# Two graph layers on one core: the order of the first batch's weight work, the bias product, the last batch's key-block sums and the last two row scalings are changed

## The chip, the cores and the metric

The kernel runs on one core of a Trainium2 chip. The metric is the device time of one execution in microseconds (us); lower is better. The engines are named as in the profile: PE is TensorE (PEld its weight loads), DVE is VectorE, ACT is ScalarE, POOL is GpSimd, SP is SyncE, which here issues most DMAs. A name with a "q" (SPq, ACTq) is the engine's sequencer, where DMA issues and waits are counted.

## The reference

The input x is 32 batches of 512 rows of 512 values; adj is one 512x512 0/1 matrix for all batches. Two layers follow one another. A layer norm here has no learned scale, and a row is normalised over its 512 values.

```python
# layer 0, per batch (a = adj as float, deg = a.sum(axis=1))
mi = x @ Wi.T ; mj = x @ Wj.T
h = layernorm(x + deg[:, None] * (mi + b) + a @ mj)
# layer 1: masked attention with 8 heads of 64
q, k, v = h @ Wq.T + bq, h @ Wk.T + bk, h @ Wv.T + bv
s = where(adj == 0, -inf, q_h @ k_h.T / 8)     # per head
o = softmax(s) @ v_h                            # heads side by side
out = layernorm(h + o @ Wo.T + bo)
```

All data are float32.

## The kernel before

**Products.** Each 512x512 product is done in seven pieces instead of eight: the weight and the activation are cut into quarters, and sums and differences of quarters are multiplied (a Strassen-like scheme). `piece` (L442) does one product of such a pair on TensorE, on one of two PSUM banks, `mma` and `mmb`; piece 1 is copied by ScalarE into `p1` (L465), and piece 2 of v and of q accumulates on the same bank afterwards, so it waits for that copy. The sums and differences of the weights' quarters are made once, by `combine` (L280), part 0 and part 1 of each weight; they are stored to DRAM (L301), and come back into a ring of seven tiles, which `prefetch` (L310) loads in the order in which the pieces will use them (L313). Each `combine` takes buffers of the pools `e` (four), `es` (two), `xa` or `oT`. Batch 0's layer 0 does not use pieces: `plain` (L629) multiplies row block ic (128 rows, ic = 0 to 3) by the whole weights, eight products of 128x128 by 512.

**The start.** `first` (L616) is an order written out by hand for batch 0 until its v, q and k begin. Its steps issue to every engine in that order, and each engine runs its own instructions strictly in order. `y[ic]` is `plain(ic)`: TensorE's product, VectorE's addition into x (L637) and statistics (L325, L326), and three small GpSimd steps (L327 to L329) that make the scale and the shift of the layer norm. `scaled(ic)` is the layer norm's scaling of that block on ScalarE (L332). `n[ic]` (`l0_norm`, L378) transposes the block on TensorE; ScalarE copies it out (L385). `half("wk", i)` is part i of the combination of k's weight on VectorE. `graph_forms(0)` and `(1)` compare adj with its transpose and sum the difference, for a flag. `fold` (L703) puts v's bias into the output bias: since the weights of a softmax sum to one, bv passes through to the product with Wo, so bo becomes bo + bv @ Wo.T. Part 0 spreads each quarter of bv over 128 columns; part 1 multiplies these four 128x128 tiles with Wo, each with 512 columns, accumulated in one PSUM tile of the pool `ov`, and VectorE adds it to `bo_r`. Behind `first` comes `phase_c(0)`: v's and q's piece 1, v's piece 2, the transposes of blocks 2 and 3, and so on.

**The batches.** From there TensorE does, in 32 periods, the attention of batch n-1 interleaved with layer 0 and projections of batches n and n-2. Per period there are eight steps, head group g (0 or 1) by key block kc (0 to 3). In each step `scores` (L508) multiplies for two head pairs (i = 0, 1) into a PSUM tile `sc` (two buffers), ScalarE takes the exponential in place (L516), and `mask` (L518) multiplies it on VectorE by the 0/1 edges into a tile `e`, of which there are four. So a mask waits until its `e` buffer was read by everybody, and scores wait until their `sc` buffer was read by the mask. `values` (L531) multiplies the masked tiles with v, in 32-column tiles; the softmax denominators come from `presum` (L523), which adds the masked tiles of successive key blocks into `es`, and from `sums` (L541), products with ones in 32-column tiles. `presum(i, kc)` with kc = 1 is line L527, with larger kc L529.

**The last batch** (`alone` in the main loop) goes step by step with little else to do. Its presums are dealt out by

```python
late = [(f, i, c, (nc.gpsimd, nc.vector)[i == c - 1]) for f, i, c in late]
```

so that of the sums at kc = 1 pair 0's is VectorE's and pair 1's is GpSimd's, and at kc = 2 the other way round; at g = 1 there are only the sums at kc = 1. One of the waiting presums is issued after each todo of the step that counts as work (`late[:1]`).

**The end.** After the last sums, the denominators are inverted by columns, the attention output is scaled, and `last_part` (L753) multiplies with Wo; block 3's product starts from x itself. `last_rows(ic)` (L766) adds, takes statistics (`ln_stats`), scales on ScalarE (L773) and stores the block (L774). `flags` (L776) makes a number that says whether the general path below has to run; all engines load it at L913.

Of the kernel before, what the change touches and what calls it, by code (L numbers as in the profile page):

```python
# [13 lines left out]
AF = mybir.ActivationFunctionType  # L14
OP = mybir.AluOpType
AX = mybir.AxisListType

P = 128
# [7 lines left out]
def gnn_attention_kernel(  # L26
# [36 lines left out]
    nc = tc.nc  # L63
    B, N, D = x.shape
    NC = N // P
    DC = D // P
# [13 lines left out]
    def work(shape, name, bufs, dtype=FT):  # L80
        return pools.work.tile(shape, dtype, name=name, bufs=bufs)
# [4 lines left out]
    def mm_tile(bank):  # L86
        return psum.tile([P, 512], FT, name="mm" + bank, bufs=1)

    def ov_tile():
        return psum.tile([P, 512], FT, name="ov", bufs=2)  # L90
# [10 lines left out]
    XT, XA, XD, AX_T, HT, MV = {}, {}, {}, {}, {}, {}  # L101
# [3 lines left out]
    def rows(ap):  # L105
        return ap.rearrange("(c p) d -> p c d", p=P)
# [35 lines left out]
    W = {}  # L142
# [9 lines left out]
    ones = const.tile([P, P], FT, name="ones")  # L152
# [77 lines left out]
    pd = mm_tile("b")  # L230
# [89 lines left out]
        return t  # L320


    def ln_stats(mv, y):
        st = work([P, 6], "st", 4)
        nc.vector.bn_stats(st, y)  # L325
        nc.vector.bn_aggr(mv[:, 0:2], st)  # L326
        nc.gpsimd.tensor_scalar(mv[:, 2:3], mv[:, 1:2], EPS, 1.0, op0=OP.add, op1=OP.mult)  # L327
        nc.gpsimd.tensor_tensor(mv[:, 3:4], mv[:, 2:3], mhalf, OP.pow)
        nc.gpsimd.tensor_scalar(mv[:, 4:5], mv[:, 0:1], mv[:, 3:4], -1.0, op0=OP.mult, op1=OP.mult)  # L329

    def ln_apply(mv, y):
        nc.scalar.activation(y, y, AF.Identity, bias=mv[:, 4:5], scale=mv[:, 3:4])  # L332
# [98 lines left out]
    OPEN = {}  # L431
# [86 lines left out]
    def mask(hp, kc):  # L518
        ps = SC.pop(hp)
        e = E[hp % 2, kc] = work([P, 2, N], "e", 4)  # L520
        nc.vector.tensor_tensor(e, ps, edge[:, kc:kc + 1, :].to_broadcast([P, 2, N]), op=OP.mult)  # L521
# [58 lines left out]
    PC, TR, GA = 1.73, 0.44, 1.9  # L580
    FLUSH = (0.0, None)

    def z(f, *a):
        return (0.0, f, *a)

    def pc(kind, b, i, bank):
        return (2 * PC if kind == "l0" else PC, piece, kind, b, i, bank)
# [5 lines left out]
    def banks(n):  # L593

        return ("a", "b") if n % 2 == 0 else ("b", "a")
# [20 lines left out]
    def first():  # L616


        g = [(GA, l0_gather, 0, dc, "ab"[dc % 2]) for dc in range(DC)]
        t = [(TR, l0_xt, 0, dc) for dc in range(DC)]  # L620
        half = lambda name, i: z(combine, name, nc.gpsimd if name in ("wi", "wj") else nc.vector, i)
        y = [(8 * PC / 4, plain, ic) for ic in range(NC)]
        n = [(TR, l0_norm, 0, ic) for ic in range(NC)]
        return [g[0], t[2], g[1], t[3], z(graph_forms, 3), g[2], g[3], half("wi", 0), z(base, 0, range(2)), z(base, 0, range(2, 4)),
                half("wv", 0), z(load_bv), half("wi", 1), z(last_load), y[0], z(scaled, 0), half("wv", 1), z(prefetch), half("wq", 0), half("wj", 0),
                z(fold, 0), y[1], z(scaled, 1), half("wq", 1), half("wj", 1), y[2], half("wk", 0), z(graph_forms, 0), z(scaled, 2), n[0],
                y[3], half("wk", 1), z(prefetch), z(graph_forms, 1), n[1], (2 * PC, fold, 1), z(scaled, 3)]

    def plain(ic):  # L629

# [72 lines left out]
    def fold(part):  # L703

        if part == 0:
            bv_w = OPEN["fold"] = work([P, DC, P], "rl", 1)
            for dc in range(DC):
                nc.vector.tensor_scalar(bv_w[:, dc, :], ones, bv_c[:, dc:dc + 1], None, op0=OP.mult)
        else:
            pd = ov_tile()  # L710
            for dc in range(DC):
                nc.tensor.matmul(pd, OPEN["fold"][:, dc, :], W["wo"][dc // 2][:, dc % 2, :], start=(dc == 0), stop=(dc == DC - 1))
            nc.vector.tensor_add(bo_r, bo_r, pd)

    def by_steps(todo, half=None):
# [23 lines left out]
    def run(f):  # L739
        f[1](*f[2:])  # L740
# [6 lines left out]
    ACC = {}  # L747
# [15 lines left out]
            nc.tensor.matmul(ACC[ic], OT[B - 1, c // 2][:, c % 2, ic * P:(ic + 1) * P], W["wo"][c // 2][:, c % 2, :],  # L763
                             start=(c == 0 and ic < NC - 1), stop=(c == 3))

    def last_rows(ic):  # L766
        y = XT[B - 1][:, ic, :]
        mv = work([P, 5], "mv", 12)
        if ic < NC - 1:
            nc.vector.tensor_add(y, y, ACC[ic])  # L770
            ACC[ic] = y
        ln_stats(mv, ACC[ic])
        nc.scalar.activation(y, ACC[ic], AF.Identity, bias=mv[:, 4:5], scale=mv[:, 3:4])  # L773
        nc.sync.dma_start(rows(out[B - 1])[:, ic, :], y)  # L774

    def flags():  # L776

        pd = ov_tile()
        nc.tensor.matmul(pd[:, 0:1], ones, tot, start=True, stop=True)
        nc.vector.tensor_scalar(tot, pd[:, 0:1], SAFE, None, op0=OP.is_lt)  # L780
        nc.vector.tensor_scalar(again, tot, -1.0, 1.0, op0=OP.mult, op1=OP.add)

    PERIODS = [first() + phase_c(0) + phase_a(1)]
    half = None
    for n in range(1, B):
        todo = phase_b(n) + phase_c(n) + phase_a(n + 1)
        if n == 1:

            a, b, c = [todo.index(f) for f in (z(between, apply, 1, 0), pc("k", 1, 2, banks(1)[0]), phase_a(2)[0])]
            PERIODS += [[todo[:a], [], todo[a:b], [], todo[b:c], [], todo[c:], []]]  # L790
            continue
        if n < B - 1:
            half = sum(f[0] for f in todo) / 2
# [13 lines left out]
    for n in range(1, B + 1):  # L807
        b = n - 1

        alone = b == B - 1  # L810
        size = 1 if alone else 2
        for step in range(0, STEPS, size):
            g, kc = divmod(step, NC)
            extra = []
            for i in range(2):
                scores(b, 2 * g + i, kc)
            for f in due:
                values(*f)
            for i in range(2):
                mask(2 * g + i, kc)  # L820
            todo = [f for todo in PERIODS[n][step:step + size] for f in todo]
            while todo and todo[0][1] is between:
                run(todo.pop(0))
            if not due:

                run(todo.pop(0))
            if due and due[-1][2] == NC - 1:
                pb, pg = due[-1][:2]
                sums(pg, *(((1, 3), 3) if pb == B - 1 else ()))
                drain(pb, pg)  # L830
                extra = rest(pb, pg)
            due = [(b, g, kc + i) for i in range(size)]
            late = [(presum, i, c) for _, _, c in due if c > 0 for i in range(2)]
            if alone:

                late = [(f, i, c, (nc.gpsimd, nc.vector)[i == c - 1]) for f, i, c in late]
                if kc > 2 - g:

                    late = []
                if g == 1 and kc == 0:  # L840

                    for f in extra[:-1]:
                        f[0](*f[1:])
                    extra = extra[-1:]
                hold = False
            else:
                for i in range(2):
                    scores(b, 2 * g + i, kc + 1)
                for f in late if kc > 0 else []:

                    if f[2] == kc:
                        f[0](*f[1:])
                late = [(mask, 2 * g + i, kc + 1) for i in range(2)] + extra[-1:] + [f for f in late if f[2] > kc]

                for f in extra[:-1] if extra else late[:1]:
                    f[0](*f[1:])
                late, extra, hold = late[0 if extra else 1:], [], bool(extra) and g == 1
            for f in todo:
                if f is FLUSH:
                    some = len(extra)  # L860
                else:
                    run(f)

                    some = 0 if f[0] == 0.0 else len(extra) if step == 0 and alone else max(1, round(f[0] / PC))
                    if f[1] is piece and f[2] == "l0" and f[4] == 3:

                        some = 0
                    if some and hold:

                        some, hold = 0, False  # L870
                if some:
                    for g in late[:1] + extra[:some]:
                        g[0](*g[1:])
                    late, extra = late[1:], extra[some:]
            for g in late + extra:
                g[0](*g[1:])
    sums(1, (1, 2), 3)
    values(B - 1, 1, 3)
    sums(1, (3,), 3)
# [26 lines left out]
    nc.vector.reduce_sum(tot, told, axis=AX.X)  # L906
    last_part(2, ic=3)
    last_part(3, ic=3)
    last_rows(2)
    last_rows(3)  # L910
    flags()
    fast.close()
    flag = nc.values_load(again[0:1, 0:1], min_val=0, max_val=1)  # L913
    with tc.If(flag > 0), tc.tile_pool(name="general", bufs=1) as pools.work:
        wi, wj, wv, wq, wk, wo = [load_w(work([P, DC, D], f"w{i}", 1), src, nc.sync)
                                  for i, src in enumerate((wiT, wjT, wvT, wqT, wkT, woT))]
# [5 lines left out]
        pd = mm_tile("a")  # L922
# [22 lines left out]
        with tc.For_i(0, B, 1) as b:  # L945
            g = "general"
# [7 lines left out]
            for ic in range(NC):  # L954
                c = slice(ic * P, (ic + 1) * P)
# [10 lines left out]
            for ic in range(NC):  # L966
                c = slice(ic * P, (ic + 1) * P)
                nc.vector.tensor_copy(V[g][:, ic, :], product([(HT[g][:, dc, c], wv[:, dc, :]) for dc in range(DC)]))
            for hp in range(HP):
                c = slice(hp * P, (hp + 1) * P)  # L970
# [5 lines left out]
                for qb in range(NC):  # L976
# [7 lines left out]
                    for s in range(2):  # L984
# [3 lines left out]
                                            op0=OP.mult, op1=OP.add)  # L988
# [11 lines left out]
                    for kc in range(NC):  # L1000
                        for s in range(2):
                            c0 = hp * P + s * HD
                            nc.tensor.matmul(pm[s * HD:(s + 1) * HD, :P], V[g][:, kc, c0:c0 + HD], pT[:, s, kc, :],
                                             start=(kc == 0), stop=(kc == NC - 1))
                    nc.scalar.copy(OT[g, hp][:, qb * P:(qb + 1) * P], pm[:, :P])
            for ic in range(NC):
                c = slice(ic * P, (ic + 1) * P)
# [45 lines left out]
```

## Time and profile before

| | |
|---|---|
| timed runs | 3634.32, 3634.50, 3635.02, 3635.49 us; median 3634.76 |
| the profiled execution | 3637.43 us, its span 3635.7 us, mean granted TensorE clock 0.999 |
| busy share of the span | PE 100%, PEld 69%, DVE 65%, POOL 55%, ACT 28% |
| sum of presums on GpSimd, 128x1024 (L527) | 126 of 2.355 us |
| mask on VectorE, 128x1024 (L521) | 512 of 1.217 us |
| one float32 piece (8 passes of 128x256) | 1.73 us from one piece's start to the next's |
| scores of both pairs (8 passes of 64x512) | 1.92 us likewise |

A float32 product shows up as two passes on PE, so four products of the program are "x8" in the profile. The duration of a merged group of matmuls (1.89 for a piece) includes the last one's way through the array; what counts for the next one is the time from start to start. The timeline gives start, duration, engine, line and operation, tiles, and in brackets how long the engine had been idle and what ended that.

### The profile page before, as it was taken

The page shows a single profiled execution, that of the slowest core. Times are in us where ns is not written, and L with a number is a line of the kernel's source. Part 1 is how long each engine was busy: PE and PEld are TensorE (multiplying, and loading weights), DVE is VectorE, ACT ScalarE, POOL GpSimd, SP SyncE. Part 2 cuts the span into 40 slices and gives each one's busy share as a digit, 9 for nine tenths or more (in the row PEclk, how much of TensorE's full clock was granted, in tenths as well). Part 3 has the DMA queues.
Part 4 walks back from the last instruction along what each step waited for, and adds up shares of the span by engine and source line. Part 5 has one row for each costly group of instructions (what it writes and reads, how often), then busy time and mean ns, then how long its engine had stood idle before and what let it go on. Part 6 is the DMA issues. An engine that isn't in the chain of part 4 may idle for free.

```text
span 3635.7 us, 49789 instructions
## 1 busy us (share of the span) xinstructions
PE 3619.5 (100%) x18480; PEld 2525.3 (69%) x18480; DVE 2377.1 (65%) x3139; ACT 1035.8 (28%) x1486; POOL 2001.2 (55%) x1981
## 2 busy tenths in 40 slices
PE   9999999999999999999999999999999999999998
PEld 6677767776777667766776677667776777677764
DVE  5566666666766666666666666666666666666666
ACT  2322232222322222223223322232222222222222
POOL 4465654656456565455564465654656555565453
PEclk9999999999999999999999999999999999999999
DMA  8445555454555445554555545555554555455541
GB/s 266 139 125 142 145 148 162 143 137 138 145 162 153 132 136 147 157 161 119 146 146 154 160 131 140 144 145 163 146 135 136 148 160 153 131 139 145 159 134 56
DMA packets 797190, 530.02 MB, mean 146 GB/s; under 512 B 530448, under 2 KB 611856, under 8 KB 796944
## 3 DMA queue, kind: packets, MB, share of 16 engines
q1 hardware_dynamic: 779200, 493.73, 49.4%
q10 hardware_dynamic: 17520, 32.51, 2.5%
q8 instruction: 150, 2.46, 0.3%
q14 instruction: 96, 0.79, 0.1%
q0 software_dynamic: 224, 0.53, 0.0%
HBM read 453.25 MB, written 73.40 MB: 145 GB/s over the span
## 4 chain that ended last, share of the span: by engine, by line
PE 97%; DVE 1%; DMA 1%; POOL 1%; ACT 0%; issue 0%; SPq 0%; ACTq 0%; POOLq 0%; DVEq 0%
PE mma L458 32%; PE mmb L458 31%; PE sc L512 13%; PE ov L538 12%; PE mmb L356 3%; PE mma L356 3%; PE sc L548 2%; DMA xh<-in_x_dram 0%; DVE rl L557 0%; DMA b_r<-in_b_dram 0%; DMA wj<-e 0%; DVE xh L376 0%; DVE e L521 0%; POOL big L427 0%; DMA ring<-in_wvT_dram 0%; POOL es L527 0%
## 5 line engine op out<-in xcount | busy, mean ns | idle before, releaser
L521 DVE TENSOR_TENSOR e<-sc,edge 128x1024 f32<-128x1024 f32 x512 | 607.2, 1217 | 493.1 <-PE ov L538 481.5
L516 ACT ACTIVATE sc<-sc 128x1024 f32<-128x1024 f32 x512 | 495.2, 1007 | 902.6 <-PE sc L512 900.0
L458 PE MATMUL mmb<-ring,big 128*128 128x256 f32 x3144 | 728.4, 380 | 0.6 <-ACT big L385 0.6
L458 PE MATMUL mma<-ring,big 128*128 128x256 f32 x3112 | 721.0, 380 | 1.3 <-ACT p L465 1.3
L458 PEld LDWEIGHTS mmb<-ring,big 128*128 128x128 f32 x3144 | 594.5, 190 | 104.9 <-issue 24.3
L458 PEld LDWEIGHTS mma<-ring,big 128*128 128x128 f32 x3112 | 588.4, 190 | 105.3 <-issue 24.1
L427 POOL TENSOR_TENSOR big<-big 128x512 f32<-128x512 f32 x376 | 488.6, 1326 | 258.7 <-PE sc L512 234.4
L512 PE MATMUL sc<-q,k 64*128 64x512 f32 x2048 | 514.7, 621 | 2.6 <-DVE e L521 2.6
L538 PE MATMUL ov<-e,v 128*32 128x512 f32 x4096 | 467.6, 596 | 0.0
L190 POOL TENSOR_TENSOR xlo<-xh,xhi 128x512 fp32r<-128x512 f32 x127 | 161.7, 1284 | 533.5 <-ACT xhi L189 533.4
L458 PE MATMUL mma<-big,ring 128*128 128x256 f32 x1808 | 428.7, 380 | 0.0
L458 PE MATMUL mmb<-big,ring 128*128 128x256 f32 x1776 | 421.3, 380 | 0.0
L458 PEld LDWEIGHTS mma<-big,ring 128*128 128x128 f32 x1808 | 341.7, 190 | 60.1 <-issue 12.1
L458 PEld LDWEIGHTS mmb<-big,ring 128*128 128x128 f32 x1776 | 335.6, 190 | 59.9 <-issue 13.0
L512 PEld LDWEIGHTS sc<-q,k 64*128 64x128 f32 x2048 | 165.5, 185 | 287.9 <-DVE e L521 146.6
L327 POOL TENSOR_SCALAR mv<-mv 128x1 f32<-128x1 f32 x256 | 79.8, 312 | 516.9 <-DVE mv L326 504.6
L538 PEld LDWEIGHTS ov<-e,v 128*32 128x32 f32 x4096 | 119.8, 110 | 328.8 <-issue 327.3
L527 POOL TENSOR_TENSOR es<-e 128x1024 f32<-128x1024 f32 x126 | 295.3, 2355 | 57.9 <-DVE e L521 57.9
L529 DVE TENSOR_TENSOR es<-es,e 128x1024 f32<-128x1024 f32 x249 | 297.3, 1215 | 0.0
L473 POOL TENSOR_TENSOR xh<-xh,p 128x512 f32<-128x512 f32 x186 | 230.6, 1268 | 110.2 <-ACT p L465 110.2
L476 DVE TENSOR_TENSOR xh<-xh,mma 128x512 f32<-128x512 f32 x186 | 126.9, 682 | 190.8 <-PE mma L458 174.4
L476 DVE TENSOR_TENSOR xh<-xh,mmb 128x512 f32<-128x512 f32 x186 | 126.9, 682 | 189.9 <-PE mmb L458 173.4
(168 smaller groups left out, 3639.4 us busy)
## 6 DMA issues: line engine op xcount, KB each, us to landing
ring<-wo SPq DMA_DIRECT2D x217, 256.0 KB, 2.8
ring<-wq SPq DMA_DIRECT2D x160, 256.0 KB, 3.6
ring<-wv SPq DMA_DIRECT2D x160, 256.0 KB, 3.2
ring<-wk SPq DMA_DIRECT2D x160, 256.0 KB, 4.5
ring<-wi SPq DMA_DIRECT2D x155, 256.0 KB, 2.6
ring<-wj SPq DMA_DIRECT2D x155, 256.0 KB, 2.6
xh<-in_x_dram SPq DMA_DIRECT2D x31, 1024.0 KB, 6.1
xa<-in_x_dram SPq DMA_DIRECT2D x124, 256.0 KB, 4.3
```

The lines of the kernel that those rows point to most:

```text
L190: (by or nc.gpsimd).tensor_sub(lo, xs, hi.bitcast(FT))
L356: nc.tensor.matmul(pm, parts[w][:, jc, :], adjR[:, jc, :], start=(w == 0 and jc == 0), stop=(w == 1 and jc == NC - 1))
L427: nc.gpsimd.tensor_tensor(dst, p, q, op=OP.subtract)
L458: nc.tensor.matmul(pm[:, c * Q:(c + 1) * Q], lhs, rhs, start=first, stop=(kc == 1 and n == len(terms) - 1), skip_group_check=True)
L473: nc.gpsimd.tensor_tensor(d, d, p1, op=OP.add)
L476: nc.vector.tensor_tensor(d, d, pm, op=OP.add)
L512: nc.tensor.matmul(ps[:, s, :], KT[b, hp // 2][r, hp % 2, kc * P:(kc + 1) * P], QT[b, hp // 2][r, hp % 2, :], start=True, stop=True)
L516: nc.scalar.activation(ps, ps, AF.Exp, scale=QSCALE)
L521: nc.vector.tensor_tensor(e, ps, edge[:, kc:kc + 1, :].to_broadcast([P, 2, N]), op=OP.mult)
L527: (by or nc.gpsimd).tensor_add(ES[i], E[i, 0], E[i, 1])
L529: (by or nc.vector).tensor_add(ES[i], ES[i], E[i, kc])
L538: nc.tensor.matmul(PV[g][r][32 * h:32 * h + 32, :], V[b][:, kc, c0:c0 + 32], E[h // 2, kc][:, h % 2, :], start=(kc == 0), stop=(kc == NC - 1))
```

## The change

1. **Order in `first`.** The two parts of the combination of k's weight and `graph_forms(1)` move to the end of the list, behind the scaling of row block 3; the second `prefetch` moves ahead of them. The bias product moves ahead of `y[3]`, and `n[1]` comes directly behind it.
2. **The bias product.** `fold(1)` no longer accumulates four products of 128 columns. Each quarter goes with 32 columns to a 32-column tile of its own, that is to 32 rows of the PSUM tile; ScalarE copies the result times 1/32 into an `es` buffer. `fold(2)` multiplies that with ones (128x128, 512 columns), which sums over the rows, and VectorE adds it to `bo_r`.
3. **The last batch's presums.** Pair 1's at g = 0, kc = 1 goes from GpSimd to VectorE; the others stay. At g = 1 both waiting presums are issued at the first occasion, so that pair 1's on GpSimd comes ahead of the layer-norm steps of batch 30's rows.
4. **The last two row blocks.** For blocks 2 and 3 GpSimd no longer makes the shift; the scaling moves from ScalarE to VectorE as (value - mean) * scale, and stands behind `flags`.

```diff
-    def ln_stats(mv, y):
+    def ln_stats(mv, y, shift=True):
...
-        nc.gpsimd.tensor_scalar(mv[:, 4:5], mv[:, 0:1], mv[:, 3:4], -1.0, op0=OP.mult, op1=OP.mult)
+        if shift:
+            nc.gpsimd.tensor_scalar(mv[:, 4:5], mv[:, 0:1], mv[:, 3:4], -1.0, op0=OP.mult, op1=OP.mult)
...
-                z(fold, 0), y[1], z(scaled, 1), half("wq", 1), half("wj", 1), y[2], half("wk", 0), z(graph_forms, 0), z(scaled, 2), n[0],
-                y[3], half("wk", 1), z(prefetch), z(graph_forms, 1), n[1], (2 * PC, fold, 1), z(scaled, 3)]
+                z(fold, 0), y[1], z(scaled, 1), half("wq", 1), half("wj", 1), y[2], z(graph_forms, 0), z(scaled, 2), n[0],
+                z(fold, 1), y[3], n[1], z(fold, 2), z(scaled, 3), z(prefetch), half("wk", 0), half("wk", 1), z(graph_forms, 1)]
...
-        else:
+        elif part == 1:
+
             pd = ov_tile()
             for dc in range(DC):
-                nc.tensor.matmul(pd, OPEN["fold"][:, dc, :], W["wo"][dc // 2][:, dc % 2, :], start=(dc == 0), stop=(dc == DC - 1))
+                nc.tensor.matmul(pd[32 * dc:32 * dc + 32, :], OPEN["fold"][:, dc, :32], W["wo"][dc // 2][:, dc % 2, :], start=True, stop=True)
+            OPEN["fold"] = work([P, 2, N], "es", 2)[:, 0, :]
+            nc.scalar.mul(OPEN["fold"], pd, 1 / 32)
+        else:
+
+            pd = ov_tile()
+            nc.tensor.matmul(pd, ones, OPEN.pop("fold"), start=True, stop=True)
             nc.vector.tensor_add(bo_r, bo_r, pd)
...
-    def last_rows(ic):
+    def last_rows(ic, apply=True):
...
-        ln_stats(mv, ACC[ic])
-        nc.scalar.activation(y, ACC[ic], AF.Identity, bias=mv[:, 4:5], scale=mv[:, 3:4])
+        MV[ic] = mv
+        ln_stats(mv, ACC[ic], shift=apply)
+        if apply:
+            nc.scalar.activation(y, ACC[ic], AF.Identity, bias=mv[:, 4:5], scale=mv[:, 3:4])
+            nc.sync.dma_start(rows(out[B - 1])[:, ic, :], y)
+
+    def last_apply(ic):
+
+        y = XT[B - 1][:, ic, :]
+        nc.vector.tensor_scalar(y, ACC[ic], MV[ic][:, 0:1], MV[ic][:, 3:4], op0=OP.subtract, op1=OP.mult)
         nc.sync.dma_start(rows(out[B - 1])[:, ic, :], y)
...
-                late = [(f, i, c, (nc.gpsimd, nc.vector)[i == c - 1]) for f, i, c in late]
+                late = [(f, i, c, nc.gpsimd if (g, i, c) in ((0, 0, 2), (1, 1, 1)) else nc.vector) for f, i, c in late]
...
-                    for g in late[:1] + extra[:some]:
-                        g[0](*g[1:])
-                    late, extra = late[1:], extra[some:]
+                    n_late = 2 if alone and g == 1 else 1
+                    for h in late[:n_late] + extra[:some]:
+                        h[0](*h[1:])
+                    late, extra = late[n_late:], extra[some:]
...
-    last_rows(2)
-    last_rows(3)
+    last_rows(2, False)
+    last_rows(3, False)
     flags()
+    last_apply(2)
+    last_apply(3)
```

More of the change, by code (lines that the diff above doesn't have):

```diff
@@ L708, in fold @@
                 nc.vector.tensor_scalar(bv_w[:, dc, :], ones, bv_c[:, dc:dc + 1], None, op0=OP.mult)
+        elif part == 1:
+            pd = ov_tile()
+            for dc in range(DC):
+                nc.tensor.matmul(pd[32 * dc:32 * dc + 32, :], OPEN["fold"][:, dc, :32], W["wo"][dc // 2][:, dc % 2, :], start=True, stop=True)
+            OPEN["fold"] = work([P, 2, N], "es", 2)[:, 0, :]
+            nc.scalar.mul(OPEN["fold"], pd, 1 / 32)
         else:
             pd = ov_tile()
-            for dc in range(DC):
-                nc.tensor.matmul(pd, OPEN["fold"][:, dc, :], W["wo"][dc // 2][:, dc % 2, :], start=(dc == 0), stop=(dc == DC - 1))
+            nc.tensor.matmul(pd, ones, OPEN.pop("fold"), start=True, stop=True)
             nc.vector.tensor_add(bo_r, bo_r, pd)
@@ L871, in gnn_attention_kernel @@
                 if some:
-                    for g in late[:1] + extra[:some]:
-                        g[0](*g[1:])
-                    late, extra = late[1:], extra[some:]
-            for g in late + extra:
-                g[0](*g[1:])
+                    n_late = 2 if alone and g == 1 else 1
+                    for h in late[:n_late] + extra[:some]:
+                        h[0](*h[1:])
+                    late, extra = late[n_late:], extra[some:]
+            for h in late + extra:
+                h[0](*h[1:])
     sums(1, (1, 2), 3)
```

## The prediction

> **What bounds it now.** I read the page first, then the chain that ended last, then the timeline of both ends and the windows of granted clock.
>
> ```profile
> span 3635.7 us, 49789 instructions
> PE 3619.5 (100%) x18480; PEld 2525.3 (69%) x18480; DVE 2377.1 (65%) x3139; ACT 1035.8 (28%) x1486; POOL 2001.2 (55%) x1981
> PE 97%; DVE 1%; DMA 1%; POOL 1%; ACT 0%; issue 0%; SPq 0%; ACTq 0%; POOLq 0%; DVEq 0%
> ```
>
> TensorE carries 97% of the chain. The change leaves TensorE's order alone between the first 60 us and the last 80 us, so only what TensorE does or waits for at these two ends can move the time. The head, from the timeline (start, duration, instruction, idle before it and who ended that):
>
> ```profile
> 47.98 3.60 PE L712 MATMUL ov<-xh,rl 128*128 128x512 f32 x8
> 48.82 0.69 DVE L290 TENSOR_TENSOR e<-q,e 128x512 f32<-128x512 f32 x1 [5.43 <-DMA wj<-e]
> 51.63 0.68 DVE L637 TENSOR_TENSOR xh<-xh,mmb 128x512 f32<-128x512 f32 x1
> 54.98 0.81 ACT L332 ACTIVATE xh<-xh,mv 128x512 f32<-128x512 f32 x1 [6.21 <-POOL mv L329]
> 55.70 0.56 ACT L465 COPY p<-mma 128x512 f32<-128x512 f32 x1
> 56.31 1.99 PE L458 MATMUL mma<-ring,big 128*128 128x256 f32 x8 [1.27 <-ACT p L465]
> ```
>
> VectorE stood 5.43 us in k's combination, for a buffer whose store had not landed. Behind it were queued the comparison (L257, 2.28) and the row-3 addition (L637), then the statistics, ScalarE's scaling (L332) and, behind that in ScalarE's order, the copy of P1 that v's second piece waits for: TensorE idle 1.27. The tail:
>
> ```profile
> 3575.82 2.35 DVE L521 TENSOR_TENSOR e<-sc,edge 128x1024 f32<-128x1024 f32 x2 [4.11 <-POOL es L527]
> 3577.09 2.26 PE L512 MATMUL sc<-q,k 64*128 64x512 f32 x8 [0.96 <-DVE e L521]
> 3605.08 1.23 DVE L521 TENSOR_TENSOR e<-sc,edge 128x1024 f32<-128x1024 f32 x1 [2.99 <-POOL es L527]
> 3606.36 1.93 PE L512 MATMUL sc<-q,k 64*128 64x512 f32 x4 [1.66 <-DVE e L521]
> 3608.22 2.77 PE L538 MATMUL ov<-e,v 128*32 128x512 f32 x16
> ```
>
> Twice in the last batch a mask waits for a GpSimd sum of key blocks that holds its buffer, and TensorE waits for the mask. After the second wait the clock falls (columns of the windows: length; busy PE, PEld, DVE, ACT, POOL; granted clock, DMA):
>
> ```profile
> 3604.00:3606.00 2.00, 0.70 (x4) 0.00 (x0) 0.92 (x1) 1.01 (x1) 1.05 (x1) 1.00 0.00 0
> 3606.00:3608.00 2.00, 1.64 (x4) 0.36 (x4) 1.93 (x6) 0.00 (x0) 0.70 (x2) 0.64 0.00 0
> 3608.00:3610.00 2.00, 2.00 (x14) 0.47 (x16) 1.66 (x2) 1.67 (x3) 1.30 (x5) 0.51 0.00 0
> 3610.00:3612.00 2.00, 2.00 (x24) 0.56 (x20) 0.59 (x1) 0.76 (x2) 0.00 (x0) 1.00 0.14 55
> ```
>
> The end is a chain of small steps to the last store:
>
> ```profile
> 3628.22 0.81 ACT L773 ACTIVATE xh<-xh,mv 128x512 f32<-128x512 f32 x1 [0.90 <-POOL mv L329]
> 3628.53 0.55 POOL L328 TENSOR_TENSOR mv<-mv,mhalf 128x1 f32<-128x1 f32 x1
> 3629.48 0.78 ACT L773 ACTIVATE xh<-sc,mv 128x512 f32<-128x512 f32 x1 [0.46 <-POOL mv L329]
> ```
>
> **Head: bias product and k's combination.** Out go eight passes of 128 columns, from 47.98 to v's first piece at 51.42: 3.44 us. In come eight passes on four 32-column tiles, then two full ones. The nearest row of the first kind is L548 (128*32, x8), where the next work starts 0.86 to 0.97 later; with a change of tile shape on both sides I take 0.95. The full product is a quarter of the old, 0.86. Net 1.6 less.
>
> The tiles now stand before row 3, so row 3 ends and the transposes of block 1 start at 47.55 + 0.95 = 48.5. They need W_o: its eight loads are issued by 35.4 and land within 4.6, at 39.6, before TensorE is there at 40.7. The added ScalarE multiply waits for the tiles; behind it stand the copy of block 1, the row-3 scaling and the P1 copies. It runs about 46.6 to 47.2 (a 128x512 copy from PSUM is 0.58, L385), even if L257, now beside row 2's small GpSimd steps, holds those back to 45.3. TensorE, with v's first piece queued behind the ones product, needs it at 48.9: free, else one for one. v's first piece starts at 49.8, its second could at 53.25 (two pieces of 1.73).
>
> What is late next is the P1 copy. Row 3's product is out at 48.66; VectorE is free (its stall is gone); addition and statistics take 1.65, as for row 2 (40.44 to 42.07). GpSimd's three small steps took 1.64 (row 3) and 2.04 (row 2, where VectorE additions of two SBUF operands ran beside them). Here k's combination runs beside them: 1.4 to 2.1. Scaling starts at 51.8 to 52.5, the P1 copy 0.72 later and the piece 0.61 after that: 53.2 to 53.85, against 56.31. I take 53.55: **2.75 less**, ends 2.4 and 3.1.
>
> k's combination itself (five steps, 3.1 us) and the sum L259 (2.28) end near 56.6, before VectorE is wanted at 63.5. On SP's queue q's ring load now passes k's five stores, which wait for VectorE until about 55.2; behind them v's next ring load, landing by 60.7 (up to 5.1 to land), is needed at 65.0. Hidden with 4 us to spare; beyond that each microsecond counts.
>
> **Tail, first wait.** The sum of head pair 1 (2.34 on GpSimd, from 3573.44) becomes a VectorE sum: 1.21 alone (3598.16), 1.75 beside GpSimd (3569.36). It starts at 3571.7 and ends by 3573.4; the masks, queued behind it, then run to 3575.85. If GpSimd's second L427 keeps going first, they run to 3577.1. TensorE reaches the scores at 3575.87 and their second half at 3576.73. Issue to issue they took 3577.09 to 3579.28; undisturbed 3575.87 to 3577.79: **1.5 less**, 1.0 if GpSimd goes first. The three following steps of VectorE and GpSimd start earlier with the masks, and the next scores have 0.6 to spare.
>
> **Tail, second wait.** The GpSimd sum is now issued before the layer-norm steps, so it starts at 3599.4 (behind VectorE's own sum, 3598.16 to 3599.37, which is issued before the mask that GpSimd waits for ends) and ends at 3601.75. Masks: to 3602.95 and 3604.15. TensorE wants the second at 3604.43. The layer-norm steps behind the sum move by 1.5, the scaling behind those holds the next exponential by 0.3; its masks end 3608.5, wanted 3609.2. Scores' second half, values, sums ran 3604.43 to 3612.53; without wait and at full clock 0.86 + 1.72 + 1.72, to 3608.73: **3.8 less**, of which 1.93 is idle and 1.87 is half clock (scores 1.86 for 0.86, values 2.59 for 1.72).
>
> [...]
>
> **End.** The two last scalings move to VectorE and two GpSimd steps of 0.26 go. Block 2 is scaled from 3627.97 instead of 3628.22, block 3's GpSimd steps start at 3627.85 and end at 3628.75, or 0.35 later if VectorE's scaling holds them as L297 held L328 (0.61 instead of 0.55, begun 0.2 before L297's end, and 1.00 beside L289). The scaling of block 3 costs 0.42 (L297, from SBUF) to 0.69 (L770, PSUM); not under 0.42, the quickest 128x512 row of VectorE. I take 0.69, as its operand is in PSUM. It ends at 3629.45 to 3629.8, against 3630.26. The load of the flag queued behind it on VectorE (0.82) ends with SP's. **0.6 less**, ends 0.45 and 0.8.
>
> **Sum.** 2.75 + 1.5 + 3.8 + 0.6 = 8.65. The profiled execution took 3637.43 (span 3635.7), the timed median is 3634.76, 2.67 lower. Profiled: 3628.8. Timed: **3626.1**.
>
> **Rivals.** *The half clock is not to be had.* Either the gap did not cause it, or the timed runs, 2.67 quicker than the profiled one, never had it. For: only one gap of three (1.27, 0.96, 1.66) was followed by it. Against: the four timed runs lie within 1.17, so its 1.87 is in all or in none. Gain 8.65 - 1.87 = 6.8: 3628.0, within 0.2%. [...]
>
> *The waits move.* At 3598.2 GpSimd's sum goes ahead of VectorE's; then masks end 3605.8, TensorE stands some 1.4 again, the clock may fall again, and the first wait keeps 0.5. Gain 4 to 6: 3629 to 3631. Against: VectorE's sum was issued 0.07 before the mask ended.
>
> *Slower.* One more allocation of the sum buffer (es) in the head swaps the two buffers in every batch. If that delayed a mask, TensorE would pay 31 times; from 0.51 us a batch (8.65 + 7.3 = 15.9) it is slower by 0.2%; at 0.6 us 3644.7. For: both waits above came through such buffers. Against: between 110 and 3550 us no mask waits for GpSimd.
>
> **Numbers.** 0.2% is 7.3 us, about what a measurement of this kernel can tell from no change. All four terms: 0.58. No half clock: 0.20. Waits move: 0.16. Slower: 0.06. Faster by over 7.3: 0.58 nearly whole (lowest sum 2.4 + 1.0 + 3.8 + 0.45 = 7.65) plus 0.04 from the second case's high end (6.8 + 0.7), 0.62; within: 0.32. The range goes from all terms at their best (9.2, with 0.5 for the spread of the timed runs) to the middle of moved waits, 4.7 less.
>
> **What would show it.** Right: v's second piece near 53.5; scores at 3575.87 less the head's gain without a VectorE wait; clock 1.00 through the last scores; the last scaling ended 0.5 sooner after the last sums. Wrong: a TensorE wait over 0.5 us in the last 60, clock still near 0.5 there, or the middle of the trace longer.

## The result and the profile after

Timed, the changed kernel takes 3629.2 us (median of 40 runs, 3628.55 to 3629.69), against 3634.82 us (median of 60, 3633.48 to 3636.72) before: 5.6 us or 0.16% less, ratio 0.9984 with a 95% interval of 0.998 to 0.9989. The forecast was 3626.1 (3625.0 to 3630.1): the right direction, inside the range, 3.1 us too low. The gain stays within the 0.2% that the prediction took for no clear change, to which it had given 0.32 against 0.62 for more. The profiled executions differ by more, 3637.43 and 3629.42, or 8.0 us. Where the other 2.4 us of that went is half of this story.

The page of after, span, busy shares and chain by engine:

```profile
span 3627.7 us, 49792 instructions
PE 3616.6 (100%) x18482; PEld 2525.1 (70%) x18482; DVE 2379.7 (66%) x3142; ACT 1034.5 (29%) x1485; POOL 2000.9 (55%) x1978
PE 99%; DVE 0%; POOL 0%; DMA 0%; issue 0%; ACT 0%; POOLq 0%; DVEq 0%
```

The chain is TensorE's to 99% (97% before): the waits at both ends are out of it. The head, from the timeline:

```profile
40.90 1.06 PE L714 MATMUL ov<-xh,rl 128*32 128x512 f32 x8
42.29 2.14 POOL L327 TENSOR_SCALAR mv<-mv 128x1 f32<-128x1 f32 x1 [1.40 <-DVE mv L326]
49.30 1.02 PE L720 MATMUL ov<-es,ones 128*128 128x512 f32 x2
50.16 1.89 PE L459 MATMUL mma<-ring,big 128*128 128x256 f32 x8
50.78 0.19 POOL L327 TENSOR_SCALAR mv<-mv 128x1 f32<-128x1 f32 x1 [5.35 <-DVE mv L326]
51.89 1.89 PE L459 MATMUL mmb<-big,ring 128*128 128x256 f32 x8
52.05 0.82 ACT L333 ACTIVATE xh<-xh,mv 128x512 f32<-128x512 f32 x1 [1.96 <-POOL mv L330]
52.78 0.56 ACT L466 COPY p<-mma 128x512 f32<-128x512 f32 x1
53.62 1.89 PE L459 MATMUL mma<-ring,big 128*128 128x256 f32 x8
```

The four 32-column products and the product with ones stand where the prediction put them. Row 3 is scaled at 52.05, the copy of P1 follows at 52.78, and v's second piece starts at 53.62, right behind the two pieces before it (50.16, 51.89) and without a wait; in before it started at 56.31 after 1.27 of idle. The tail:

```profile
3569.46 1.70 DVE L528 TENSOR_TENSOR es<-e 128x1024 f32<-128x1024 f32 x1
3573.90 1.99 PE L513 MATMUL sc<-q,k 64*128 64x512 f32 x8
...
3594.69 1.21 DVE L528 TENSOR_TENSOR es<-e 128x1024 f32<-128x1024 f32 x1
3594.85 3.28 POOL L528 TENSOR_TENSOR es<-e 128x1024 f32<-128x1024 f32 x1 [14.11 <-DVE e L522]
3598.16 2.36 DVE L522 TENSOR_TENSOR e<-sc,edge 128x1024 f32<-128x1024 f32 x2 [0.64 <-POOL es L528]
3600.11 1.99 PE L513 MATMUL sc<-q,k 64*128 64x512 f32 x8
```

Both groups of scores (3573.90, 3600.11) now run without a break. GpSimd's sum starts beside VectorE's, takes 3.28 instead of 2.35, and still ends before TensorE wants the mask. The granted clock is 1.00 in every 2 us window from 3598 to 3606. The end:

```profile
3620.82 0.54 DVE L789 TENSOR_SCALAR xh<-xh,mv 128x512 f32<-128x512 f32 x1
3621.14 0.63 POOL L328 TENSOR_TENSOR mv<-mv,mhalf 128x1 f32<-128x1 f32 x1
3621.80 0.81 DVE L789 TENSOR_SCALAR xh<-sc,mv 128x512 f32<-128x512 f32 x1 [0.44 <-POOL mv L328]
```

Step by step between the two traces: the first sums of the batches start at 147.53 instead of 150.34 (2.81 less). The lead falls to 2.17 by the last batch. The first wait's end adds 1.30, the second's 3.58, and the last scaling ends at 3622.61 instead of 3630.26, 0.60 more: 7.65.

### The profile page after: what moved, and what is told of

Its sections match the earlier page's. It is cut to its first block, busy times and chain, and to the rows that moved or that the text cites. A ratio compares the mean times of both kernels' runs of the same rounds, so it can differ in the third digit from the quotient of the medians.

```text
span 3627.7 us, 49792 instructions
## 1 busy us (share of the span) xinstructions
PE 3616.6 (100%) x18482; PEld 2525.1 (70%) x18482; DVE 2379.7 (66%) x3142; ACT 1034.5 (29%) x1485; POOL 2000.9 (55%) x1978
## 4 chain that ended last, share of the span: by engine, by line
PE 99%; DVE 0%; POOL 0%; DMA 0%; issue 0%; ACT 0%; POOLq 0%; DVEq 0%
PE mma L459 32%; PE mmb L459 32%; PE sc L513 14%; PE ov L539 13%; PE mmb L357 3%; PE mma L357 3%; PE sc L549 2%; PE mmb L636 0%; PE mma L636 0%; DMA big<-in_adj_dram 0%; PE mma L771 0%; PE sc L771 0%; DVE st L325 0%; PE sc L204 0%; PE sc L385 0%
```

## The experiments

Two questions were open: why the timed runs gained 2.4 us less than the profiled ones, and where 0.64 of the lead went in the middle, where the change touches nothing. Each kernel was timed in 11 runs, beside runs of before on the same chip; one of the 11 is its profiled execution.

**One part at a time.** The diffs are the parts of the change shown above: `e1_head` has parts 1 and 2, `e2_sums` part 3, `e3_end` part 4. `e4_sum_0` has of part 3 only the line

```diff
-                late = [(f, i, c, (nc.gpsimd, nc.vector)[i == c - 1]) for f, i, c in late]
+                late = [(f, i, c, nc.gpsimd if (g, i, c) in ((0, 0, 2), (1, 1, 1)) else nc.vector) for f, i, c in late]
```

> Parts 1 and 2 alone (order of the first batch's weight work and the bias product). Theory A, the profile's terms carry over to the timed runs one for one: v's second piece starts near 53.6 and the timed median is 2.8 us lower than before. Theory B, the stall of VectorE for the store that had not landed (5.43 us in the profile of before) is partly the profiler's own: then only the shorter bias product is gained in the timed runs, 1.6, up to 2.8. Both leave the two waits of the last batch and its time as before; the timed runs still scatter up to about 1.9 above their main group.

> Part 3 alone (the last batch's key-block sums). Theory A, the half clock behind the second wait is in every run: timed median 4.9 us lower (1.3 first wait, 1.7 to 1.9 second wait, 1.9 half clock). Theory B, the half clock is in the profile of before and in about one timed run in seven: timed median 3.0 to 3.2 lower, and the upper group of the timed runs of before (about 1.9 above the rest) is gone. Both: the trace shows no VectorE wait ahead of the last scores and the clock at 1.00 behind them.

> Part 4 alone (last two row blocks scaled by VectorE). Both theories: timed median 0.6 us lower (0.95 if the last store's landing is also quicker by the 0.35 that the two traces show); waits of the last batch and the scatter of the timed runs as before.

> Of part 3 only the sum of pair 1 at g = 0, kc = 1 goes to VectorE; at g = 1 the sums are issued one by one as before. Both theories: the first wait (0.96) goes, timed median 1.3 us lower (1.0 if VectorE's sum beside GpSimd's is slower), the second wait of TensorE (1.66, from 0.27 more) stays. Theory B: about one timed run in seven still lies some 1.9 above the rest; theory A: one group only.

| | median, us | before beside it | difference |
|---|---|---|---|
| parts 1 and 2 | 3633.50 | 3634.90 | -1.4 |
| part 3 | 3631.50 | 3634.90 | -3.4 |
| part 4 | 3634.53 | 3634.90 | -0.4 |
| part 3, first sum only | 3633.70 | 3634.90 | -1.2 |

The parts add up to 5.2 of the 5.6; each interval of a ratio is about 0.0009 wide on both sides (3.3 us), so the split rests on the traces and the medians only support it. Parts 1 and 2 came out below both theories (2.8; 1.6 to 2.8). Part 3 came out near theory B's 3.0 to 3.2. Its reason shows in the profile of `e1_head`, where the second wait is still there. The timeline, TensorE behind that wait:

```profile
3603.75 1.13 PE L512 MATMUL sc<-q,k 64*128 64x512 f32 x4 [1.67 <-DVE e L521]
3604.81 1.92 PE L538 MATMUL ov<-e,v 128*32 128x512 f32 x16
```

The same wait as in before (1.67, there 1.66), and the scores take 1.13 instead of 1.93, the values 1.92 instead of 2.77: full clock. So it is in `e3_end` (wait 1.67, scores 1.13) and in `e6_fold` (below; wait 1.66, scores 1.13), too. A kernel with this wait thus runs with the half clock in some executions and without it in others. How often can only be judged by the times, since the mean clock kept of a timed run (three digits) is too coarse. Of all 147 timed runs of before, 19 lie over 1.1 above the median of their set, about one in eight; of the 73 of the four kernels without that wait (after, `e2_sums` and two below), one does. The share is not the same in every kernel with the wait: five of the 11 runs of `e1_head` lie 0.8 to 1.5 above its median, none of `e3_end` does. Nor is a long time proof of the half clock: the profiled execution of `e6_fold` took 3636.29 and ran at full clock there (granted clock 1.00 in every 2 us window from 3600 to 3614); its head was late. Compared directly, the stretch from the last half of the scores to the sums took 4.45 in before (3606.36 to 3610.81) and 2.80 in `e1_head` (3603.75 to 3606.55): the half clock is worth 1.65 where it occurs, and going by the times the median run of before is one without it.

The 1.4 of parts 1 and 2 is half of the 2.81 that the two profiles show at the head. The profile of `e3_end`, whose head is that of before, has two rows that explain some of it (timeline, the stall and v's second piece):

```profile
47.82 0.69 DVE L290 TENSOR_TENSOR e<-q,e 128x512 f32<-128x512 f32 x1 [4.85 <-DMA wj<-e]
55.33 1.99 PE L459 MATMUL mma<-ring,big 128*128 128x256 f32 x8 [0.71 <-ACT p L466]
```

VectorE stood 4.85 there and TensorE 0.71. Over six profiled runs with the old order and the old product, TensorE's wait was 1.27, 0.58, 0.71, 0.83, 0.73 and 0.91. The profile of before had the longest of them, and its time, 3637.43, lies above all 147 timed runs. The first sums of the batches start at 149.58 on average in these six and at 147.29 in four with the new head: 2.3 gained, not 2.8. With 0.64 given back later (below), 1.65 is left, against 1.4 timed; the middle of the six lower runs of `e1_head`, 3633.17, is 1.7 below before. Whether the profiler lengthens the stall, as theory B had it, was not tested by itself; the profiled execution of `e1_head` took 3633.45, next to its median of 3633.50.

**The order alone and the product alone.** In `e5_order` the product stays as it was, and only its place and k's combination move; in `e6_fold` the product is split as in the change, with part 0 of k's combination ahead of it and part 1 right behind `y[3]`. In `e5_order` part 0 also leaves the line above the one shown, as in the change.

```diff
 e5_order
...
-                y[3], half("wk", 1), z(prefetch), z(graph_forms, 1), n[1], (2 * PC, fold, 1), z(scaled, 3)]
+                y[3], n[1], z(fold, 1), z(scaled, 3), z(prefetch), half("wk", 0), half("wk", 1), z(graph_forms, 1)]
 e6_fold
...
-                y[3], half("wk", 1), z(prefetch), z(graph_forms, 1), n[1], (2 * PC, fold, 1), z(scaled, 3)]
+                z(fold, 1), y[3], half("wk", 1), z(prefetch), z(graph_forms, 1), n[1], z(fold, 2), z(scaled, 3)]
```

> Part 1 alone: k's combination behind row 3, the bias product still four full products of 128 columns (behind block 1's transposes). TensorE's idle ahead of v's second piece should be gone (1.27 in the profiled run of before, 0.58 to 0.83 in three other profiled runs with the same head), the 1.6 of the shorter product not gained: timed median 0.6 to 1.3 lower. If the reordering, and not the shorter product, is what drops one VectorE semaphore instruction, the two masks of batches 13 and 27 start 0.35 late as in after, and 0.65 of it is given back: 0.0 to 0.6 lower.

> Part 2 alone: the bias product on 32-column tiles before row 3, its second half behind block 1's transposes; k's combination where it was before. TensorE is through with the product 1.6 earlier, but v's second piece waits for ScalarE's copy of P1, which stands behind the scaling that VectorE's stall holds: the 1.6 becomes a longer wait at that place (some 2.4 instead of 0.8), timed median as before, 0.0 to 0.3 lower; were the product itself the bound, 1.6 lower. The two late masks of after appear only if this kernel, too, has a VectorE instruction fewer (then 0.65 higher).

`e5_order`: 3634.22 against 3634.79, 0.6 less, and its trace shows no wait ahead of v's second piece. `e6_fold`: 3635.31 against 3634.96, 0.35 more, ratio 1.0002 (0.9993 to 1.0011), so no difference. Its timeline says why the shorter product alone brings nothing:

```profile
49.38 0.69 DVE L290 TENSOR_TENSOR e<-q,e 128x512 f32<-128x512 f32 x1 [6.69 <-DMA wj<-e]
52.93 1.99 PE L458 MATMUL mmb<-big,ring 128*128 128x256 f32 x8 [1.70 <-DVE xh L637]
56.88 1.99 PE L458 MATMUL mma<-ring,big 128*128 128x256 f32 x8 [1.96 <-ACT p L465]
```

TensorE comes sooner and then stands twice: q's piece waits 1.70 for the row-3 addition that frees its bank, v's second piece 1.96 for the copy of P1. Both hang on VectorE's stall. This execution is one of the five slower of its 11 (3636.29 to 3637.19; the other six 3634.38 to 3635.31), and its stall of 6.69 is longer than any of the six above, so the waits of a middle run are probably shorter; by the median they still take the whole gain. The two edits need each other.

**What was lost in the middle.** Matched matmul by matmul, after falls back by 0.3 at two places, batches 13 and 27. `e1_head` and `e5_order` fall back at the same two, `e2_sums`, `e3_end`, `e4_sum_0` and `e6_fold` nowhere. At both, a mask starts 0.35 later behind the values that free its buffer. VectorE, counted in the trace with its semaphore instructions, has one instruction fewer in the head of those three (the new order leaves one semaphore instruction out). So two kernels were made that only put instructions back:

```diff
+    PAD = [const.tile([P, 1], FT, name="pad%d" % i) for i in range(1)]        # e9_pad2: range(2)
...
-                z(fold, 1), y[3], n[1], z(fold, 2), z(scaled, 3), z(prefetch), half("wk", 0), half("wk", 1), z(graph_forms, 1)]
+                z(fold, 1), y[3], n[1], z(fold, 2), z(scaled, 3), z(prefetch), half("wk", 0), half("wk", 1), z(graph_forms, 1)] + [z(pad, i) for i in range(1)]
...
+    def pad(i):
+        nc.vector.memset(PAD[i], 0.0)
```

> After, plus one VectorE instruction that does nothing of use (a memset of 128x1 into a tile that nobody reads) at the end of the head. Theory A, code position: the change has one VectorE instruction fewer ahead of the batches (its semaphore instruction near 107 is gone), so that two masks come to stand just behind a step of 128 instructions and start 0.41 instead of 0.07 behind their wait; one instruction more puts them back: both masks start on time, TensorE gets 0.65 back, timed median 0.65 below after (about 6.2 to 6.3 below before). Theory B, the two delays come from buffers or transfers that the new order moves: time as after or 0.1 longer.

> After, plus two such VectorE instructions. Theory A: no mask of batches 13 and 27 is late, but the masks that start near 1018 and 2560 in before's time (VectorE's records 1086 and 2750 there) are, by 0.34 each: timed median as after, 0.65 above the kernel with one instruction more. Theory B: as after, with the delays in their old places near 1494 and 3039.

`e8_pad1` takes 3628.41 (3628.12 to 3628.89), 6.4 below the runs of before beside it, ratio 0.9982 (0.9973 to 0.9991); `e9_pad2` takes 3629.04 (3628.72 to 3629.75). One useless instruction gains 0.8 against after, and the second loses 0.63 again. The intervals overlap, so the traces carry this: matched matmul by matmul, `e8_pad1` falls back nowhere and `e9_pad2` by 0.3 at each of two new places. `e8_pad1` has the lowest median of all kernels here. The timeline of after, of `e8_pad1` and, at another place, of `e9_pad2`; in each the values, and the mask that waits for their first half:

```profile
1490.43 3.64 PE L539 MATMUL ov<-e,v 128*32 128x512 f32 x32
1492.81 2.35 DVE L522 TENSOR_TENSOR e<-sc,edge 128x1024 f32<-128x1024 f32 x2 [7.21 <-PE ov L539]
```
```profile
1490.12 3.64 PE L540 MATMUL ov<-e,v 128*32 128x512 f32 x32
1492.15 2.36 DVE L523 TENSOR_TENSOR e<-sc,edge 128x1024 f32<-128x1024 f32 x2 [6.85 <-PE ov L540]
```
```profile
1013.13 3.64 PE L540 MATMUL ov<-e,v 128*32 128x512 f32 x32
1015.55 2.35 DVE L523 TENSOR_TENSOR e<-sc,edge 128x1024 f32<-128x1024 f32 x2 [2.95 <-PE ov L540]
```

From the start of the values to the mask: 2.38 in after, 2.03 in `e8_pad1`, and in `e9_pad2` 2.42 at a mask that is on time in the other two (2.06). That mask and the one near 2557 are the two that theory A had named ahead of the run.

**The half clock.** `e7_sum_twice` is before with the sum that TensorE waits for made twice, `e10_sum_half` with half of it made twice.

```diff
                     for g in late[:1] + extra[:some]:
                         g[0](*g[1:])
+                        if alone and step >= NC and g[0] is presum and g[1] == 1:
+                            nc.gpsimd.tensor_add(ES[1], E[1, 0], E[1, 1])       # e10_sum_half: [:, 0, :] of each
...                                                                             # the same two lines behind the loop over the rest
```

> Before, with GpSimd's last sum of key blocks issued twice (the same sum into the same buffer), so that TensorE's second wait of the last batch grows from 1.66 by about 2.35 to about 4.0. Theory A, the clock falls behind idle gaps beyond some length: every run has the half clock behind this gap, some 4 us of it, timed median 2.35 + 1.9 = 4.2 higher, one group of times. [...] Theory C, the gap has nothing to do with it: 2.35 higher and as seldom a second group as in before.

> Before, with half of GpSimd's last sum of key blocks (128x512) made a second time: TensorE's second wait grows from 1.66 to about 2.85. [...]

`e7_sum_twice` takes 3639.07 against 3634.79, 4.3 more, all 11 runs from 3638.26 up, which is 3.5 above the median of before: the gap, longer by 2.4, does not explain that alone, so every run seems to have had the half clock. Its windows (length; busy PE, PEld, DVE, ACT, POOL; granted clock, DMA):

```profile
3604.00:3606.00 2.00, 0.00 (x0) 0.00 (x0) 0.00 (x0) 0.63 (x1) 1.99 (x1) 0.86 0.00 0
3606.00:3608.00 2.00, 0.33 (x2) 0.34 (x4) 1.61 (x2) 0.00 (x0) 0.35 (x1) 0.50 0.00 0
3608.00:3610.00 2.00, 2.00 (x8) 0.37 (x10) 1.93 (x5) 0.21 (x1) 1.20 (x4) 0.50 0.00 0
3610.00:3612.00 2.00, 2.00 (x12) 0.39 (x8) 1.50 (x2) 2.00 (x3) 0.82 (x2) 0.50 0.00 0
3612.00:3614.00 2.00, 2.00 (x24) 0.53 (x20) 0.06 (x1) 0.22 (x1) 0.00 (x0) 0.93 0.41 158
```

The clock falls inside the gap (at 3605.44, when TensorE had been idle for 1.87) and stays at half for 6.84 us; in before it was 3.40, half as long. `e10_sum_half` takes 3637.73 against 3634.96, with its gap at 3.00 instead of the expected 2.85: three runs lie 0.8 to 1.7 above before, eight 2.5 to 3.9. The longer gap alone makes 1.3 (3.00 less 1.66), with the half clock's 1.65 it is 3.0; by this estimate most runs had the half clock and some had not. But the two groups are not sharply apart, since a space as wide as the one between them (0.8) lies within the upper eight. The profiled execution (3637.87) had it: its clock fell 0.04 after the end of the gap and stayed at half for 3.40.

## Why the prediction was right or wrong

**Head, 2.75 predicted.** The main step was right: VectorE's stall ahead of row 3 is gone, and with it TensorE's wait. That v's second piece came at 53.62 against 53.55 is luck in part. The prediction let the copy of P1 set it. In the trace that copy, 52.78 and 0.56 long, was through at 53.34, and the piece began when TensorE had done the two before it: TensorE's own work was the limit. The first of these came at 50.16 instead of 49.8, since the bias product saved 1.39 and not 1.6 (from the transposes of block 0 to v's first piece 9.79, in before 11.18). On the other path two misses offset one another: the row-3 addition began at 49.07 instead of 48.66, and GpSimd's three small steps took 1.24 (50.78 to 52.02) instead of 1.4 to 2.1, so that the scaling began at 52.05, inside the forecast of 51.8 to 52.5. At row 2 alone one of these steps was long, 2.14, beside VectorE's comparison (42.12, 2.26 long). The size was read off one profile, in which the stall was the longest of six. Against their mean the term is 2.3.

**"Only what TensorE does or waits for at these two ends can move the time".** This failed. The middle got 0.64 longer, since the new order has one VectorE instruction fewer and all later ones stand one place sooner. The rival "slower" asked for a price per batch from the `es` buffers; there was none. `e8_pad1` shows that the cost is one of position.

**First wait, 1.5 predicted.** 1.30 measured (1.2 timed in `e4_sum_0`). GpSimd did not delay the masks. The prediction let TensorE reach the scores 1.73 behind the piece ahead of them; a piece followed by scores takes 1.93 (3571.97 to 3573.90 in after), and the 0.2 is what is missing.

**Second wait, 3.8 predicted.** In the profiled pair 3.58, by the path that was named: VectorE's sum first, GpSimd's ahead of the layer norm, masks in time. GpSimd's sum, though, ran beside VectorE's and not behind it: it began 0.16 later and took 3.28 instead of 2.35. It ended 3.44 after VectorE's had begun, forecast 3.59; the two misses offset one another. Of the 3.58, 1.65 is half clock, not 1.87: at full clock the second half of the scores takes 1.06 (3603.75 to 3604.81 in `e1_head`), not 0.86. That "the four timed runs lie within 1.17, so its 1.87 is in all or in none" was sound, but the term of 3.8 took it for all: judged by the times it is in about one run of eight, and then most sets of four hold none. The rival "the half clock is not to be had", at 0.20, describes the median; its 3628.0 is 1.2 off for the other reasons above. In the profiled execution of before the clock fell behind a gap of 1.66; in those of `e1_head` (1.67) and `e6_fold` (1.66) it stayed at 1.00.

**End, 0.6 predicted.** 0.60 in the traces, scaling from PSUM 0.81, forecast 0.69, with GpSimd's 0.63 under VectorE's first scaling; 0.4 timed in `e3_end`.

**The sum.** Predicted 8.65. For the timed median 2.3 - 0.65 + 1.3 + 1.93 + 0.6 = 5.5; measured 5.6. The difference of 3.2 is half clock 1.87, middle 0.65, head 0.45, first wait 0.2. That the time still lies inside the range is owed to the range's upper end, which was drawn for another reason, waits that move.

## What to carry to other kernels

A profile is one execution: before a term is taken from it, ask which of its rows differ between executions (a store's landing, a granted clock), and take the profile's surplus over the timed median, here 2.67, as a warning that some of them did. When two traces differ by a constant and then by another, match them matmul by matmul, and look for the instruction that came late with its wait unchanged. A shorter product gains nothing while its successor waits for another engine's stall; here the order had to change with it.

## What the runs showed of the hardware

**Where VectorE's instructions stand in the code.** In each of the twelve traces there are some 244 places between the head and the last few instructions where VectorE stood over 0.2 us at a single semaphore instruction between two working ones. The gap from it to the second of these is 0.045 us at nearly all of them, and 0.40 at these, counted from 0 along VectorE with its semaphore instructions: number 831 in before, in `e8_pad1` and in the six experiments that keep before's count up to there; 1599 and 3263 in after, `e1_head` and `e5_order`; 1087, 2751, 3007 and 3135 in `e9_pad2`. All leave 63 when divided by 128. (The one other long gap, 3.2, in the seven traces that have the last batch's first wait, is at the mask of that wait, which waits for GpSimd as well.) The delay cost time only where TensorE waited for that instruction: at 831, late in before and on time in after, and at the last two of `e9_pad2`, the lead does not change. What fills the 0.40 is not shown. Of the queue q14 (96 packets on the page of before, kind instruction) no packet starts inside the 0.40 at any of the 18 places; its next one starts 0.65 to 1.82 after the late instruction did.

**The clock.** The half clock lasted 3.40 us in before and `e10_sum_half` and 6.84 in `e7_sum_twice` (from the windows: twice the share that is missing to 1.00, times 2 us, summed). By the same count it began 0.20 after the end of the gap of 1.66 in before, 0.04 after the end of the gap of 3.00 in `e10_sum_half`, and at 3605.44 in `e7_sum_twice`, 1.87 into the gap of 4.09. After gaps of 1.67 in `e1_head` and `e3_end` and of 1.66 in `e6_fold` the clock did not fall. The length of the idle alone thus does not decide; what does is not shown.
